# A GNN stack under a list scheduler: layers without order between groups, other ranks, the last groups' steps alternating, and attention terms written to DRAM element by element

## The chip, the cores and the metric

The kernel runs on one core of a Trainium2 chip. The time is device microseconds of one execution. The kernel before takes 1331.21 us, the median of three runs (1329.94 to 1332.13 us).

A core has TensorE (PE, matrix products into PSUM; its weight loads are PEld), VectorE (DVE), ScalarE (ACT), GpSimd (POOL) and SyncE (SP), which here issues nearly all DMAs. Each engine executes its own instructions in the order in which the program holds them and waits on semaphores for the others.

## The reference

128 graphs of 64 nodes with 256 features go through four layers, each after a layer norm and a ReLU, each added to its input:

```python
h = jnp.maximum(_layernorm(x, axis=-1), 0.0)
x = x + _L0_gnn_ref(h, adj, W, a_src, a_dst)    # attention, 4 heads of 64
h = jnp.maximum(_layernorm(x, axis=-1), 0.0)
x = x + _L1_gnn_ref(h, adj, W, a)               # attention, 1 head of 256
h = jnp.maximum(_layernorm(x, axis=-1), 0.0)
x = x + _L2_gnn_ref(h, ...)                     # relational convolution; adj holds only 0 and 1
h = jnp.maximum(_layernorm(x, axis=-1), 0.0)
x = x + _L3_gnn_ref(h, adj, ...)                # gated graph recurrence, 3 steps of a GRU
```

An attention layer forms, for every pair of nodes of a graph and every head, the exponential of a leaky ReLU of the sum of a source term and a destination term, masks it by the adjacency, and averages the neighbours' features with it. A step of the recurrence is

```python
m = h @ weight[i]; aggr = A.T @ m               # per graph
r = sigmoid(i_r + h_r); z = sigmoid(i_z + h_z)  # i_* from aggr @ w_ih.T, h_* from h @ w_hh.T
n = tanh(i_n + r * h_n)
h = (1.0 - z) * n + z * h
```

## The kernel before

**Tiles and stages.** Two graphs fill the 128 partitions; four such pairs are a group, so there are 16 groups (NG). A group first goes through three layers (first_layer, second_layer, third_layer) and then through the three steps of the recurrence. A step (g, i) is step i of group g. A step has 42 products of 128x128 by 256 columns: for each gate a 2x2 block product is done with seven products instead of eight (class Sevens), so POOL forms sums of blocks of the state (hS) and of the aggregated state (aS). PSUM banks "sy" (two) and "sz" (three) hold the results; VectorE and ScalarE empty them. Everything else uses three banks called "mt".

**Who sets the order.** Nothing is emitted as it is written. Every call to an engine is recorded (Plan.note), belongs to a job (Plan.begin, with a start and an end in the plan's own time and a list of jobs that must have ended before), and has a planned cost (the function cost). Plan.emit then makes list schedules: forward takes, among the operations that can start, the one with the smallest due time; backward sets new due times from the end. Of 21 such passes (PASSES) the shortest in the plan's own time is emitted: that fixes the order on each engine. Where the plan leaves TensorE idle in its first 115 us, emit puts filler products "sz<-warm" (L1582).

**Order of steps.** The list steps interleaves two neighbouring groups: (g, 0), (g-1, 2), (g, 1), ... It ends with (14,0), (13,2), (14,1), (15,0), (14,2), (15,1), (15,2). The function when gives each place a slot, and a group's layers end before its first slot. The layers' jobs are chained through users: layer i of a group starts in the plan only when layer i of the group before has ended.

**The way back of the state.** A step leaves the state hT with features on partitions; the next needs it with nodes on partitions too (hnat). If the same group's next step follows at once ("quick"), TensorE transposes it: eight products "tp<-ident,hT" (back). If not, back_by_dma has VectorE transpose 32x32 blocks (tb), writes them to DRAM (way) and reads them back (hnat). The last step of all (final, in_parts) transposes on TensorE, adds the input and stores.

**Attention terms.** For each node and head, fs holds an exponential of the source term, with nodes on partitions. The pair products need it along the free axis in all partitions of the graph (t). From group 2 on (AHEAD) TensorE transposes fs (tp<-ident,fs), VectorE copies it out of PSUM (fT), one DMA writes it to DRAM rows (row<-fT, 32 or 8 pieces of 256 bytes), and two DMAs read the rows, broadcast over 64 partitions, as t. VectorE then multiplies t by gd, takes the maximum with fd and the minimum with the mask mt; TensorE aggregates (mm<-wh,t and mn<-wh,t).

Of the kernel before, what the change touches and what calls it, by code (L numbers as in the profile page):

```python
# [2 lines left out]

# [6 lines left out]
F32 = mybir.dt.float32  # L10
I32 = mybir.dt.int32
AF = mybir.ActivationFunctionType
# [209 lines left out]
class Plan:  # L222
# [54 lines left out]
            b.ops.append(op)  # L277
        return op

    PASSES, SEED, SPREAD = 21, 28, 50.0  # L280
    LEEWAY = {"PE": 100.0, "DVE": 100.0, "Activation": 100.0, "Pool": 100.0, "SP": 300.0, "-": 0.0}
    OVERLAP = {"DVE": 83.0, "Activation": 95.0, "Pool": 43.0}
    ISSUE, TURN = 665.0, 197.0
# [133 lines left out]
    def backward(self, end):  # L417
# [26 lines left out]
        for _ in self.ops:  # L444
# [14 lines left out]
            for other in before[op]:  # L459
                limit(other, op.due - self.LATENCY - other.took)  # L460

    def emit(self):

        self.on = False
        self.link()
        best, self.random = None, Random(self.SEED)
        for _ in range(self.PASSES):
            end, order = self.forward()
            if best is None or end < best[0]:
                best = end, [(op, op.start, op.idle, op.places) for op in order]  # L470
            self.backward(end)
        self.ends = best[0]
        for op, start, idle, places in best[1]:
            op.start = start
            if op.engine == "PE" and self.spare and start < 115.0 * 1e3:
                for _ in range(int((idle - 100.0) / 220.0)):
                    self.spare()
            for b, tag in places:
                b.pool.make(b, tag)
            op.call()  # L480
        self.ops = []
        return best[0]
# [46 lines left out]
def cost(engine, method, args, kwargs):  # L529

    n = elements(args[0])
    if engine == "tensor":
        m = elements(args[2] if method == "matmul" else args[0])
        return (m / 1.2 + 2.5) * (1 if method == "transpose" else 2)
    if engine == "sync" or method == "dma_start":
        to, of = args[:2]
        rate = {"way": 450.0, "fine": 175.0}.get(to.base.tag, 150.0) if isinstance(to, View) else 150.0
        if isinstance(of, View) and of.base.tag in ("way", "fine"):
            rate = 150.0 if of.base.tag == "way" else 100.0
        return n * to.shape[0] * 4 / rate  # L540
    if engine == "vector":
        if method == "bn_stats":
            return 400.0
        if method == "tensor_reduce":
            n = elements(args[1])
        plain = method == "tensor_scalar" and not any(isinstance(a, View) for a in args[2:4])
        return 150.0 + n * (0.53 if plain and n >= 512 else 1.04)
    if engine == "scalar":
        return 150.0 + 0.86 * n if method in ("copy", "mul") else 310.0 + 0.73 * n
    if ALU.pow in args:  # L550
        return 1000.0
    return 200.0 + 2.1 * n if method != "memset" else 100.0 + 0.85 * n
# [3 lines left out]
def kernel(  # L556
# [368 lines left out]
    class Recurrence:  # L925
# [7 lines left out]
        def at(self, x, k, h):  # L933

            return chunk(x, k)[:, 2 * h : 2 * h + 2]
# [69 lines left out]
        def step(self, i, back=True, in_parts=False):  # L1005
# [73 lines left out]
            def gates(c):  # L1079
                g = Sevens(c, "r", (0, 1))  # L1080
                rs, zs = (turned_part(name) for name in "rz")
                r, z = ([x[:, 2 * h : 2 * h + 2] for h in range(2)] for x in (rs, zs))

                def r_there(h, y):
                    nc.scalar.activation(r[h], y, AF.Tanh, bias=brz[:, c : c + 1], scale=0.5)
                    nc.vector.scalar_tensor_tensor(t[c][h], r[h], 1.0, t[c][h], op0=ALU.add, op1=ALU.mult)

                def z_there(h, y):
                    nc.vector.tensor_tensor(z[h], y, z[h], ALU.add)
                    if h == 0:  # L1090
                        nc.scalar.activation(zs, zs, AF.Tanh, bias=brz[:, 2 + c : 3 + c], scale=0.5)

                nc.scalar.copy(r[0], g.mul("y", 1))
                nc.vector.tensor_tensor(r[0], g.mul("m", 2), r[0], ALU.add)
                r_there(0, r[0])
                nc.scalar.copy(z[0], g.mul("y", 6))
                nc.scalar.copy(z[1], g.mul("y", 5))
                z_there(1, g.mul("z", 7))
                r_there(1, g.mul("y", 3))
                z_there(0, g.mul("z", 4))  # L1100
                return r, z, rs, zs
# [5 lines left out]
            def from_a(gated):  # L1107
                n = Sevens(0, "n", (1,))

                def add(c, h, y):  # L1110
                    nc.vector.tensor_tensor(t[c][h], t[c][h], y, ALU.add)

                def there(c, h):
                    d, z, ds, zs = gated[c]
                    nc.scalar.activation(t[c][h], t[c][h], AF.Tanh, bias=bi[:, 4 + c : 5 + c])
                    nc.gpsimd.tensor_tensor(d[h], at(hT, c, h), t[c][h], ALU.subtract)

                add(0, 0, n.mul("y", 1))
                add(0, 0, n.mul("m", 2))
                there(0, 0)  # L1120
                add(1, 0, n.mul("y", 6))
                add(1, 1, n.mul("y", 5))
                add(1, 1, n.mul("z", 7))
                there(1, 1)
                add(0, 1, n.mul("y", 3))
                there(0, 1)
                done(*gated[0][2:], chunk(hnew, 0))
                if back:
                    back_first()
                add(1, 0, n.mul("z", 4))  # L1130
                there(1, 0)
                done(*gated[1][2:], chunk(hnew, 1))

            def back_first():
                self.hT = hnew
# [23 lines left out]
    with ExitStack() as s1:  # L1159
# [47 lines left out]
        class Layer:  # L1207
# [2 lines left out]

            place = {"em": "hn", "dg": "hn", "tb": "hn", "land": "hn"}

            shared = {"hn": 3, "o": 2, "st": 4, "mv": 4, "var": 4, "rstd": 4, "nm": 4, "rec": 4, "fT": 1}

            def __init__(self, layer, pool, bufs):
                self.layer, self.pool, self.bufs = layer, pool, bufs
# [106 lines left out]
        def attention(g, p0, n, layer, heads, we, pool):  # L1323
# [13 lines left out]
            if g < AHEAD:  # L1337

                dg = pool.tile([P, nh, N], F32, name="dg")
                nc.gpsimd.tensor_tensor(  # L1340
                    dg.rearrange("p (g h) i -> p g h i", g=n),
                    diag[:, None, None, :].to_broadcast([P, n, heads, N]),
                    es[:, :, :heads, None].to_broadcast([P, n, heads, N]),
                    ALU.mult,
                )
                step = 512 // N
                for c in range(0, nh, step):
                    m = min(step, nh - c)
                    pe = psum.tile([P, 512], F32, name="mm")
                    nc.tensor.matmul(  # L1350
                        pe[:, : m * N], same, dg[:, c : c + m, :].rearrange("p c i -> p (c i)"), start=True, stop=True
                    )
                    nc.scalar.activation(
                        t[:, c : c + m, :].rearrange("p c i -> p (c i)"), pe[:, : m * N], AF.Exp, scale=ALPHA - 1.0
                    )
            else:

                fs = pool.tile([P, n, heads], F32, name="fs")
                nc.scalar.activation(fs, es[:, :, :heads], AF.Exp, scale=ALPHA - 1.0)
                pt = psum.tile([P, T], F32, name="tp")  # L1360
                nc.tensor.transpose(pt[:nh, :P], fs.rearrange("p g h -> p (g h)"), ident)
                fT = pool.tile([nh, P], F32, name="fT")
                nc.vector.tensor_copy(fT, pt[:nh, :P])
                row = dram.tile([2, nh * N], F32, name=f"row{layer}")
                nc.sync.dma_start(row.rearrange("a (c i) -> c a i", i=N), fT.rearrange("c (a i) -> c a i", i=N))
                for half in range(2):
                    nc.sync.dma_start(
                        t[half * N : (half + 1) * N].rearrange("p c i -> p (c i)"),
                        row[half : half + 1, :].to_broadcast([N, nh * N]),
                    )  # L1370
# [113 lines left out]
        start, slot = 87.96, 27.0  # L1484
        PLAIN = (0, NG - 1)
        steps = [(0, 0), (0, 1)]
        for g in range(1, NG):
            steps += [(g, 0), (g - 1, 2), (g, 1)]
        steps.append((NG - 1, 2))
        turn = {step: n for n, step in enumerate(steps)}  # L1490

        def when(g, i):
            return start + turn[g, i] * slot

        users = {}

        def layers_of(g):
            if g > 1:
# [11 lines left out]
            for p0, n, at in units:  # L1510
                spare = g == 0 and p0 > 0
                for i in range(3):
                    end = None if g < 2 else at[i + 1]
                    nc.begin((g, p0, i), at[i], end, [users[i]] if i in users and not spare else [])
                    if g > 1:
                        nc.job.spread = 3.0
                    if not spare:
                        users[i] = (g, p0, i)
                    layers[i](g, p0, n, spare)
            if g == 0:  # L1520
                nc.begin("make")
# [278 lines left out]
```

## The time and the profile before

| | us |
|---|---|
| median of the runs | 1331.21 |
| profiled execution | 1333.37 |
| its span, first to last instruction | 1331.6 |
| TensorE busy in the span | 1307.7 |
| VectorE busy | 1065.1 |
| ScalarE busy | 859.2 |
| GpSimd busy | 691.5 |
| DMA of queue q1, share of 16 engines | 34.8% |

The span is cut into 40 equal slices; a digit is the busy share of a slice in tenths, and PEclk is the granted clock of TensorE:

```profile
PE   9998999999999999999999999999999999999986
PEld 8666877878788787878778787877878788778875
DVE  6578688897979788796988879697897979777663
ACT  4866667676676767666676666766676666655543
...
PEclk9999999999999999999999999999999999999998
DMA  7110224435343534524253443434335323422210
```

A float32 product shows as two records. Records overlap, since a product's end is modelled, so the distance from one start to the next says more than a record's length. A group of instructions is named output<-inputs with buffer numbers left out; nearly all come from one helper (L495), so groups are told apart by their tiles. "Landing" is the time from a DMA's issue to its end.

### The profile page before, as it was taken

The page shows a single profiled execution, that of the slowest core. Times are in us where ns is not written, and L with a number is a line of the kernel's source. Part 1 is how long each engine was busy: PE and PEld are TensorE (multiplying, and loading weights), DVE is VectorE, ACT ScalarE, POOL GpSimd, SP SyncE. Part 2 cuts the span into 40 slices and gives each one's busy share as a digit, 9 for nine tenths or more (in the row PEclk, how much of TensorE's full clock was granted, in tenths as well). Part 3 has the DMA queues.
Part 4 walks back from the last instruction along what each step waited for, and adds up shares of the span by engine and source line. Part 5 has one row for each costly group of instructions (what it writes and reads, how often), then busy time and mean ns, then how long its engine had stood idle before and what let it go on. Part 6 is the DMA issues. An engine that isn't in the chain of part 4 may idle for free.

```text
span 1331.6 us, 27942 instructions
## 1 busy us (share of the span) xinstructions
PE 1307.7 (98%) x9889; PEld 1039.4 (78%) x9889; DVE 1065.1 (80%) x2556; ACT 859.2 (65%) x2173; POOL 691.5 (52%) x845
## 2 busy tenths in 40 slices
PE   9998999999999999999999999999999999999986
PEld 8666877878788787878778787877878788778875
DVE  6578688897979788796988879697897979777663
ACT  4866667676676767666676666766676666655543
POOL 2664553655565355554645455654555546453642
PEclk9999999999999999999999999999999999999998
DMA  7110224435343534524253443434335323422210
GB/s 215 28 36 25 80 85 152 123 101 166 104 124 96 157 114 125 155 94 133 84 159 112 124 148 103 134 98 151 100 115 164 101 90 91 142 66 56 98 54 20
DMA packets 132061, 143.90 MB, mean 108 GB/s; under 512 B 43336, under 2 KB 117320, under 8 KB 131912
## 3 DMA queue, kind: packets, MB, share of 16 engines
q1 hardware_dynamic: 131352, 141.50, 34.8%
q8 instruction: 81, 1.33, 0.4%
q14 instruction: 68, 0.56, 0.1%
q10 hardware_dynamic: 560, 0.52, 0.1%
HBM read 80.48 MB, written 60.96 MB: 106 GB/s over the span
## 4 chain that ended last, share of the span: by engine, by line
PE 93%; DVE 3%; ACT 2%; POOL 1%; issue 0%; DMA 0%; SPq 0%; DVEq 0%; POOLq 0%
PE sy L495 37%; PE sz L495 28%; PE mm L495 17%; PE mm L787 4%; PE tp L787 3%; PE sz L1582 2%; PE tp L495 1%; DVE hT L495 1%; PE tq L787 1%; ACT hn L495 1%; DVE r L495 0%; PE mn L787 0%; DVE t L495 0%; DVE st L495 0%; ACT z L495 0%
## 5 line engine op out<-in xcount | busy, mean ns | idle before, releaser
L495 POOL TENSOR_TENSOR r<-hT,hT 128x256 f32<-128x256 f32 x192 | 152.2, 799 | 266.1 <-ACT hT L495 265.2
L495 DVE SCALAR_TENSOR_TENSOR hT<-r,hT 128x256 f32<-128x256 f32 (+1 forms) x288 | 181.6, 635 | 39.2 <-ACT r L495 37.0
L495 PE MATMUL sy<-hS,wsum 128*128 128x256 f32 x576 | 173.4, 384 | 1.0 <-ACT z L495 0.6
L495 PE MATMUL sy<-aS,wsum 128*128 128x256 f32 x576 | 173.0, 383 | 0.0
L495 PE MATMUL sz<-hS,whh 128*128 128x256 f32 x576 | 170.5, 383 | 0.1
L495 PE MATMUL sz<-aS,wc 128*128 128x256 f32 x576 | 164.7, 383 | 0.0
L495 DVE TENSOR_TENSOR hT<-hT,sz 128x256 f32<-128x256 f32 x288 | 118.2, 411 | 54.7 <-PE sz L495 48.3
L495 POOL TENSOR_TENSOR aS<-aT 128x256 f32<-128x256 f32 x96 | 80.9, 843 | 150.8 <-ACT aT L495 150.6
L495 ACT ACTIVATE hT<-sy,bh 128x256 f32<-128x256 f32 x192 | 90.6, 472 | 68.8 <-PE sy L495 66.4
L495 PEld LDWEIGHTS sy<-hS,wsum 128*128 128x128 f32 x576 | 107.1, 191 | 30.3 <-issue 8.8
L495 ACT ACTIVATE hT<-hT,bi 128x256 f32<-128x256 f32 x192 | 95.3, 505 | 50.9 <-DVE hT L495 49.5
L495 PEld LDWEIGHTS sz<-hS,whh 128*128 128x128 f32 x576 | 107.1, 190 | 23.2 <-issue 7.4
L495 PEld LDWEIGHTS sy<-aS,wsum 128*128 128x128 f32 x576 | 107.2, 190 | 19.7 <-issue 3.2
L495 PEld LDWEIGHTS sz<-aS,wc 128*128 128x128 f32 x576 | 106.5, 190 | 18.4 <-issue 1.2
L495 POOL TENSOR_TENSOR rstd<-var,mhalf 128x4 f32<-128x4 f32 (+1 forms) x70 | 74.9, 1070 | 82.6 <-ACT var L495 78.1
L495 PE MATMUL mm<-wl,hT 128*128 128x512 f32 x248 | 117.5, 593 | 0.0
L495 ACT ACTIVATE hn<-xg,nm,rstd 128x256 f32<-128x256 f32 x200 | 107.2, 593 | 10.7 <-POOL nm L495 10.2
L495 ACT COPY z<-sy 128x256 f32<-128x256 f32 x192 | 70.7, 369 | 66.4 <-PE sy L495 65.0
L495 DVE TENSOR_TENSOR hT<-hT,sy 128x256 f32<-128x256 f32 x192 | 79.6, 414 | 32.6 <-PE sy L495 30.2
L495 DVE TENSOR_TENSOR z<-sz,z 128x256 f32<-128x256 f32 x192 | 79.7, 416 | 32.3 <-PE sz L495 27.5
L495 DVE SCALAR_TENSOR_TENSOR r<-z,r 128x512 f32<-128x512 f32 x96 | 89.0, 929 | 13.8 <-ACT z L495 7.6
L495 DVE BATCH_NORM_STATS2 st<-xg 128x6 f32<-128x256 f32 x256 | 95.8, 409 | 3.2 <-DMA xg<-in_x_dram 3.1
(207 smaller groups left out, 3228.7 us busy)
## 6 DMA issues: line engine op xcount, KB each, us to landing
way<-tb SPq DMA_DIRECT2D x58, 512.0 KB, 2.7
hnat<-way SPq DMA_DIRECT2D x180, 128.0 KB, 2.9
way<-hn SPq DMA_DIRECT2D x42, 512.0 KB, 3.0
hn<-way SPq DMA_DIRECT2D x168, 128.0 KB, 3.0
xg<-in_x_dram SPq DMA_DIRECT2D x15, 512.0 KB
out_dram<-xg SPq DMA_DIRECT2D x15, 512.0 KB, 2.9
t<-row SPq DMA_DIRECT2D x28, 256.0 KB, 4.0
hT<-way SPq DMA_DIRECT2D x52, 128.0 KB, 2.6
```

Of the source, the lines that this page charges most:

```text
L495: return do(*[real(a) for a in args], **{k: real(v) for k, v in kwargs.items()})
L787: nc.nc.tensor.matmul(*[real(x) for x in product], start=True, stop=True)
L1582: nc.spare = lambda: psum.spare and nc.nc.tensor.matmul(pause, warm, warm, start=True, stop=True)
```

## The change

It does six things.

- The list users is gone: a layer's job no longer waits for the same layer of the group before.
- The last steps alternate: (14,0), (13,2), (15,0), (14,1), (15,1), (14,2), (15,2). No step of group 15 follows another of it at once, so (15,1) brings its state back by DMA and not on TensorE.
- Due times are shifted: 50 passes and not 21, from another seed; then 125 recorded random moves (MOVES), each of which shifts the due times of some jobs, in a stretch of the plan, on some or all engines, and one more forward pass whose order is emitted.
- Planned costs of DMAs of the tags "way" and "fine" are other numbers.
- In the last step, the tanh of z and the function done work on halves (256 columns) instead of on both at once (512).
- From group 2 on, fs goes to the DRAM rows straight from its 128 partitions: two DMAs, one for each graph of the pairs, in which every element is a piece of 4 bytes (1024 pieces each in the first layer, 256 in the second). The transposes of fs, the copies fT and their tile are gone.

```diff
-    PASSES, SEED, SPREAD = 21, 28, 50.0
+    PASSES, SEED, SPREAD = 50, 3, 50.0
+    MOVES = (
+        3000014, 3000022, 3000028, 3000041, 3000063, 3000064, 3000083, 3000087, 3000102, 3000106, 3000107, 3000112,
...
+    RANKED = ("PE", "DVE", "Activation", "Pool", "SP")
+
+    def move(self, seed, end, jobs):
...
+        u()
+        middle = u() * end
+        width = (15e3 if u() < 0.5 else 50e3) * (0.3 + u())
+        by = (60.0, 200.0, 600.0, 2000.0)[int(u() * 4)]
+        together = int(u() * 3) == 0
+        for j in jobs:
+            if not abs(j.sum / j.count - middle) < width or u() < 0.5:
+                continue
+            if together:
+                d = shift(by)
+                for e in self.RANKED:
+                    j.shift[e] += d
+            else:
+                for e in self.RANKED:
+                    if u() >= 0.5:
+                        j.shift[e] += shift(by)
...
         for _ in range(self.PASSES):
+            ranks = [op.due for op in self.ops]
             end, order = self.forward()
             if best is None or end < best[0]:
-                best = end, [(op, op.start, op.idle, op.places) for op in order]
+                best = end, ranks, [op.start for op in self.ops]
             self.backward(end)
+        end, ranks, starts = best
...
+        for m in self.MOVES:
+            self.move(m, end, jobs)
+        for op, due in zip(self.ops, ranks):
+            op.due = due + op.job.shift.get(op.engine, 0.0)
+        end, order = self.forward()
+        best = end, [(op, op.start, op.idle, op.places) for op in order]
...
-        rate = {"way": 450.0, "fine": 175.0}.get(to.base.tag, 150.0) if isinstance(to, View) else 150.0
+        rate = {"way": 450.0, "fine": 220.0}.get(to.base.tag, 150.0) if isinstance(to, View) else 150.0
         if isinstance(of, View) and of.base.tag in ("way", "fine"):
-            rate = 150.0 if of.base.tag == "way" else 100.0
+            rate = 170.0 if of.base.tag == "way" else 125.0
...
                     nc.vector.tensor_tensor(z[h], y, z[h], ALU.add)
-                    if h == 0:
+                    if in_parts:
+                        nc.scalar.activation(z[h], z[h], AF.Tanh, bias=brz[:, 2 + c : 3 + c], scale=0.5)
+                    elif h == 0:
                         nc.scalar.activation(zs, zs, AF.Tanh, bias=brz[:, 2 + c : 3 + c], scale=0.5)
...
                     nc.gpsimd.tensor_tensor(d[h], at(hT, c, h), t[c][h], ALU.subtract)
+                    if in_parts:
+                        done(d[h], z[h], t[c][h])
...
-                done(*gated[1][2:], chunk(hnew, 1))
+                if not in_parts:
+                    done(*gated[1][2:], chunk(hnew, 1))
...
-                pt = psum.tile([P, T], F32, name="tp")
-                nc.tensor.transpose(pt[:nh, :P], fs.rearrange("p g h -> p (g h)"), ident)
-                fT = pool.tile([nh, P], F32, name="fT")
-                nc.vector.tensor_copy(fT, pt[:nh, :P])
                 row = dram.tile([2, nh * N], F32, name=f"row{layer}")
-                nc.sync.dma_start(row.rearrange("a (c i) -> c a i", i=N), fT.rearrange("c (a i) -> c a i", i=N))
+
+                def scatter():
+                    with nc.allow_non_contiguous_dma(reason="attention terms to rows"):
+                        for a in range(2):
+                            nc.sync.dma_start(
+                                real(row)[a].rearrange("(c i) -> i c", i=N),
+                                real(fs)[a * N : (a + 1) * N].rearrange("p g h -> p (g h)"),
+                            )
+
+                nc.note("SP", scatter, 150.0 * nh, [row], [fs], dma=True)
...
-        for g in range(1, NG):
+        for g in range(1, NG - 1):
             steps += [(g, 0), (g - 1, 2), (g, 1)]
-        steps.append((NG - 1, 2))
+        steps[-1:] = [(NG - 1, 0), (NG - 2, 1), (NG - 1, 1), (NG - 2, 2), (NG - 1, 2)]
...
-        users = {}
-
...
-                    nc.begin((g, p0, i), at[i], end, [users[i]] if i in users and not spare else [])
+                    nc.begin((g, p0, i), at[i], end)
                     if g > 1:
                         nc.job.spread = 3.0
-                    if not spare:
-                        users[i] = (g, p0, i)
```

Counted in the built programs, TensorE loses 28 transposes of fs, 8 of the state and 18 filler products (106 to 88), VectorE loses 28 copies, gains two block transposes and has eight half-size operations in place of four whole ones, and SP has 33 DMAs more.

## The prediction

> **What bounds the kernel now.** I read the page's busy shares first, then the windows of the span, then TensorE's timeline where a window was not full.
>
> ```profile
> PE 1307.7 (98%) x9889; PEld 1039.4 (78%) x9889; DVE 1065.1 (80%) x2556; ACT 859.2 (65%) x2173; POOL 691.5 (52%) x845
> ...
> 0.00:99.60 99.60, 96.78 (x671) 73.09 (x671) 63.27 (x189) 64.10 (x203) 47.52 (x88) 1.00 0.33 93
> ...
> 126.20:136.20 10.00, 5.89 (x33) 3.95 (x36) 9.93 (x20) 6.53 (x14) 9.86 (x10) 0.92 0.00 0
> 136.20:1292.50 1156.30, 1153.42 (x8788) 922.01 (x8788) 952.36 (x2257) 761.01 (x1895) 613.95 (x721) 1.00 0.37 115
> 1292.50:1304.30 11.80, 8.19 (x88) 6.62 (x88) 4.96 (x7) 4.51 (x10) 5.88 (x8) 0.71 0.14 46
> ```
>
> From 136 to 1292 us TensorE is busy for 1153.4 of 1156.3 us: there only less TensorE work makes the kernel faster. Time that isn't work lies at three places: before the first recurrence product, in the turn from step (0,0) to (0,1), and in the turn from (15,1) to (15,2). TensorE's timeline shows the last of them, and the form list shows three groups that only fill or move data:
>
> ```profile
> 1296.28 1.09 PE L495 MATMUL tp<-ident,hT 128*128 128x128 f32 x4 [3.61 <-DVE hT L495]
> 1297.16 1.91 PE L495 MATMUL sy<-hT,whh 128*128 128x256 f32 x4
> ...
> 1303.30 0.70 PE L495 MATMUL sy<-hS,wsum 128*128 128x256 f32 x2
> ...
> L1582 PE MATMUL sz<-warm 128*128 128x128 f32 x212 | 29.3, 289 | 1.1 <-DVE warm L1580 1.1
> ...
> L495 PE MATMUL tp<-ident,fs 128*16 128x128 f32 x14 | 3.8, 273 | 0.0
> L495 PE MATMUL tp<-ident,fs 128*4 128x128 f32 x14 | 3.8, 273 | 0.0
> ```
>
> TensorE waits 3.61 us for VectorE's state, and then four records take 1.91 us where elsewhere eight take 1.73: the bubble is followed by products at half rate.
>
> **What the Trainium skill says.** "TensorE: Matmul & The Clock Gate", "What's actually happening": after an idle window of about 3.4 us the clock falls to half until a busy window has passed. The trace agrees: after the 3.61 us bubble a record's pitch is about 0.43 us until about 1302, against 0.216. "DMA: Bandwidth & Descriptors", "Rules for kernel authors": a last dimension that is not contiguous gives one descriptor per element, and "Specifications" there names read-modify-write below 512 B. The one such transfer of before, the two bias loads (1536 pieces of 4 bytes around 27 us), shows no such penalty on reads; 4-byte writes to DRAM don't occur in before.
>
> ```profile
> DMA packets 942, 0.01 MB, mean 13 GB/s; under 512 B 942, under 2 KB 942, under 8 KB 942
> ## 3 DMA queue, kind: packets, MB, share of 16 engines
> q1 hardware_dynamic: 942, 0.01, 86.8%
> ...
> DMA to landing us min/median/max: 1.3/1.3/2.2
> ```
>
> The first three lines are 27.0 to 27.6 us: 942 packets in 0.6 us on 16 engines is one per 16 x 600 / 942 = 10.2 ns and engine. The last is row<-fT, 32 pieces of 256 bytes in layer 0 and 8 in layer 1.
>
> **The change, part by part.** A 256-wide record has a pitch of 0.216 us (eight in 1.73), a product has two; a 128-wide transpose has (1.09 - 0.27) / 7 = 0.117 us (eight hn transposes at 129.97).
>
> 1. *Rows without TensorE.* From group 2 on, 28 transposes of fs leave TensorE: 28 x 0.117 = 3.3 us, in the stretch that is full, so it counts in full. VectorE loses 28 copies of 272 ns, 7.6 us of an 80% busy engine. SP gets 28 more issues; a bias issue with 768 pieces took 516 ns. Chain: in layer 0 of the 14 visits, read off the timeline, the row issue came 2.2 us after fs started (TensorE, then VectorE had to get to it), the issue of t 1.8 us later, 3.9 together. Now: fs 0.23 and a hop of 0.1, first issue 0.52, then for the second half 64 pieces per engine at 10.2 ns, 0.65, and the 1.3 us of row<-fT: 2.8 us, about 1 us earlier. Write pieces are the unknown: at the read price the chain gains, and it is neutral at (3.9 - 1.6) / 128 = 18 ns a piece. I take the read price, since 256-byte row writes also land in 1.3 us, and book the shorter chain at nothing: products of t follow 14 to 18 us of other products in both orders. SP's queue behind the wait for fs holds way<-tb and hnat<-way of the running recurrence, as it did behind fT.
>
> 2. *Last steps alternate.* Before, (15,1) and (15,2) follow each other. From 1292.5 to 1304.3 TensorE has 88 records: 64 of the aggregation (one burst of about 1.1 us), 8 transposes, 16 records of 0.216 = 3.5 us. Useful 4.6 of 11.8 us; lost 7.2, transposes and half clock included. Now (14,2) with 42 products, 42 x 0.43 = 18 us, lies between, and the state returns by DMA: two block transposes (0.7 us each), way and hnat (2.7 and 2.9 us to landing), under 10 us with issues. It fits, as it does in every earlier step, so I count 7.2 us. What is late next is group 15's layers, wanted a slot earlier; in the new order their last products stand at 1095 us of TensorE work against 1109 before, so they have moved along.
>
> 3. *New order at the head.* Summing products at their pitches over the two built orders, the first recurrence product stands after 66.8 us of work and 106 filler products (0.222 us each, 23.5 us) before, and starts at 99.6: 9.3 us are neither. After the change it stands behind 76.4 us of work and 88 fillers, 19.5 us. Fillers are put where the plan has TensorE idle. With the same 9.3 us the head loses 28.8 instead of 32.8: 4.0 us gained.
>
> 4. *Turn (0,0) to (0,1).* 126.2 to 136.2 us: 12 records of 0.216 and 16 transposes make 4.5 us of work in 10 us, 5.5 lost. In the new order eight hn transposes and five w1e products (0.9 + 2.2 us) stand ahead of the first state product, and three more w1e products and a layer-0 aggregation (1.3 + 0.6 us) ahead of the last four state transposes. I take 4.0 of the 5.5.
>
> 5. *The last step in halves.* Tanh of z on 256 columns instead of 512 saves 0.2 us, and two VectorE operations of 0.69 become 0.43 each; but a 0.68 us hnat addition now stands ahead of the last one on VectorE. 0.3 us.
>
> 6. *Layers free of each other, shifted ranks, "fine" rates.* No tile has the tag "fine"; the way rate only moves the order. In the full stretch nothing can be gained but the 3 us of gaps; new orders bring waits of their own. Before has five gaps of 0.7 to 1.4 us from one product to the next there (at 193, 685, 929, 1023 and 1090 us); I book 3 us more, between -3 and +8.
>
> Sum: -3.3 - 7.2 - 4.0 - 4.0 - 0.3 + 3.0 = -15.8. The profiled execution was 1333.4 us with a span of 1331.6, so 1.8 lie around it; the median of the runs, 1331.2, is 2.2 below it. 1331.2 - 15.8 = 1315.
>
> **The rivals.**
> - *The model's fill does not come (items 3 and 4 fail).* Fillers are placed by the kernel's own plan, not by a measurement; loads and VectorE could be late as before. For: VectorE is 9.93 of 10 us busy in the turn at 126 us, so it may still decide there. Against: layer products that need nothing of it stand in between now. Then -3.3 - 7.2 - 0.3 + 3 = -7.8: 1323.
> - *The 4-byte writes are slow: slower than before.* Place: VectorE's first multiplication of t, which waits for t<-row; behind it stand the recurrence's PSUM readers, then TensorE. Price: each ns per piece beyond 18 costs 128 x 14 = 1.8 us over the 14 layer-0 visits. At 18 + 15.8 / 1.8 = 27 ns the gain is gone, at 28 the kernel is 0.2% slower, at 40 ns it takes 1331 - 16 + 40 = 1355. For: all pieces of one column lie side by side in the same lines of DRAM, written by all engines, and the skill's read-modify-write. Against: the read price of 10 ns, and a 256-byte write's quick landing.
> - *New waits eat the gain.* Freed layers crowd the buffers; 16 us over 1156 us would be one 0.25 us gap per 18 us. Against: TensorE's products still have 14 us of others ahead of them. 1331.
>
> **How the numbers follow.** Main case 0.61, at 1315, own range 1308 to 1321 (items 2 to 4 all full, or interior +8). First rival 0.21, at 1323. Slow writes 0.12. Eaten 0.06. A measurement of this kernel can tell 0.2%, 2.7 us: faster is the main case and the first rival, 0.82; same 0.06; slower 0.12. The range leaves out the slow writes and a little at each end: 1306 to 1330.
>
> **What would show it.** In the new profile: no tp<-ident,fs and no fT; row<-fs landing in 2 to 3 us after its issue; 0 to 100 us with 76 us of work before the first sy product at about 104 us; no gap over 1 us with half clock between 1270 and the last step; VectorE's waits for t<-row at a few us in all, as the 1.7 us before. Wrong would be: waits for t<-row of tens of us and DMA shares near full around row<-fs (slow writes), or the middle stretch under 99% busy (new waits).

## The result and the profile after

The changed kernel takes 1516.82 us (median of five runs, 1514.23 to 1519.35) beside 1330.83 for the kernel before (five runs in turn with it, 1329.94 to 1332.13): a ratio of 1.1397, interval 1.1381 to 1.1414. It is 14% slower; the forecast was 1315.

The page of the profile after, its busy times, its slices, its DMA queues and its chain of work that ended last:

```profile
PE 1363.2 (90%) x9817; PEld 1067.0 (70%) x9817; DVE 1068.8 (70%) x2534; ACT 858.6 (57%) x2173; POOL 698.7 (46%) x845
...
PE   9988897988988889798887988789898997989997
...
q1 hardware_dynamic: 167968, 142.55, 36.4%
...
PE 61%; DMA 19%; DVE 9%; ACT 4%; issue 4%; POOL 2%; SPq 1%; another core or an unknown queue 0%; DVEq 0%; ACTq 0%; POOLq 0%
PE sy L553 23%; PE sz L553 18%; PE mm L553 12%; DMA row<-fs 10%; DMA t<-row 4%; DMA way<-tb 3%; PE mm L845 3%; DVE hT L553 2%; DVE t L553 2%; PE tp L845 2%; SPq L553 1%; PE sz L1647 1%; ACT hT L553 1%; PE tp L553 1%; DMA xg<-in_x_dram 1%
```

(The helper is L553 now, the aggregation L845.) VectorE, ScalarE and GpSimd have nearly the same work as before. The DMA engines' share is hardly higher (q1 36.4% of the span beside 34.8%), and yet DMA holds 19% of the chain, where it held 0% before. One window of the span, first of the kernel before, then of the changed one, gives the place; the columns are the busy times of PE, PEld, DVE, ACT and POOL with their instructions, PEclk, DMA share and GB/s:

```profile
136.20:1275.00 1138.80, 1135.92 (x8707) 906.88 (x8708) 940.58 (x2231) 753.31 (x1878) 606.62 (x714) 1.00 0.38 115
136.20:1275.00 1138.80, 1011.02 (x7332) 790.38 (x7331) 795.40 (x1868) 642.33 (x1609) 513.39 (x600) 0.93 0.39 98
```

In this stretch TensorE is idle for 127.8 us, where it was for 2.9 us before, and its granted clock is 0.93 on average. Bubbles are followed by half clock, and here it doesn't take one of 3.4 us, the figure that the prediction cites: around a bubble of 2.48 us (263.2 to 265.7 us) the clock is 0.50 from 265.4 to 268.8. The waits name the transfer (us in total, times, longest): VectorE's for t, then those in SyncE's queue for the rows, each before (L495) and after (L553):

```profile
DVE t L495 <- DMA t<-row: 1.7, 4, 0.7
DVE t L553 <- DMA t<-row: 122.5, 23, 15.0
...
SPq L495 <- DMA row<-fT: 24.4, 23, 2.9
SPq L553 <- DMA row<-fs: 202.9, 32, 10.5
```

SyncE's timeline shows one visit of each attention layer, first one of layer 1 (two writes of 256 pieces), then one of layer 0 (two of 1024); the columns are start, length and tiles:

```profile
319.89 1.25 SPq L553 DMA_DIRECT2D row<-fs  x2
321.25 0.55 SPq L553 DMA_DIRECT2D way<-tb  x1
...
329.84 2.22 SPq L553 DMA_DIRECT2D t<-row  x2
332.17 1.00 SPq L553 DMA_DIRECT2D hnat<-way  x2
...
350.71 1.34 SPq L553 DMA_DIRECT2D row<-fs  x2
361.97 1.13 SPq L553 DMA_DIRECT2D t<-row  x2
```

The reads of t are issued 10.0 and 11.3 us after the first of the rows' writes; in the first visit the state's way back, hnat<-way, stands behind them in the same queue. In the visit of layer 0 the DMA engines are not at work all that time. The DMA line of the window 350.7 to 362 us, in 40 slices of 0.28 us:

```profile
DMA  0000276573000000000000000000050000000000
...
q1 hardware_dynamic: 2080, 0.01, 8.2%
```

The 2048 pieces go through the engines between 352.0 and 353.4 us. The queue's next transfer is issued only 8.6 us later (the mark in between is a fetch of instructions): the writes are through the engines but have not landed. In the visit of layer 1 a write of the state, way<-tb, was issued behind the pieces, and there the engines do show as busy (319.8 to 330 us):

```profile
DMA  0230040043999990000000900000168431140666
...
q1 hardware_dynamic: 1109, 0.62, 79.2%
```

The 128 packets of 4096 bytes in this window, the state's, take 0.91 us each on average; such packets take 0.18 us in the kernel before. So other writes behind the pieces are slow as well.

### The profile page after: what moved, and what is told of

Same layout as the page of the kernel before. It is cut to its first block, busy times and chain, and to the rows that moved or that the text cites. A ratio compares the mean times of both kernels' runs of the same rounds, so it can differ in the third digit from the quotient of the medians.

```text
span 1517.5 us, 27822 instructions
## 1 busy us (share of the span) xinstructions
PE 1363.2 (90%) x9817; PEld 1067.0 (70%) x9817; DVE 1068.8 (70%) x2534; ACT 858.6 (57%) x2173; POOL 698.7 (46%) x845
## 3 DMA queue, kind: packets, MB, share of 16 engines
q1 hardware_dynamic: 167968, 142.55, 36.4%
## 4 chain that ended last, share of the span: by engine, by line
PE 61%; DMA 19%; DVE 9%; ACT 4%; issue 4%; POOL 2%; SPq 1%; another core or an unknown queue 0%; DVEq 0%; ACTq 0%; POOLq 0%
PE sy L553 23%; PE sz L553 18%; PE mm L553 12%; DMA row<-fs 10%; DMA t<-row 4%; DMA way<-tb 3%; PE mm L845 3%; DVE hT L553 2%; DVE t L553 2%; PE tp L845 2%; SPq L553 1%; PE sz L1647 1%; ACT hT L553 1%; PE tp L553 1%; DMA xg<-in_x_dram 1%
## 5 line engine op out<-in xcount | busy, mean ns | idle before, releaser
L553 POOL TENSOR_TENSOR r<-hT,hT 128x256 f32<-128x256 f32 x192 | 152.2, 799 | 364.1 <-ACT hT L553 359.4
L553 PE MATMUL sy<-aS,wsum 128*128 128x256 f32 x576 | 184.8, 407 | 30.5 <-DVE hT L553 26.4
L553 DVE SCALAR_TENSOR_TENSOR hT<-r,hT 128x256 f32<-128x256 f32 (+1 forms) x290 | 183.7, 637 | 24.1 <-ACT r L553 21.9
L553 PE MATMUL sy<-hS,wsum 128*128 128x256 f32 x576 | 179.4, 397 | 9.7 <-ACT z L553 6.9
L553 PE MATMUL sz<-hS,whh 128*128 128x256 f32 x576 | 178.4, 395 | 8.2 <-DVE hT L553 4.1
L553 PE MATMUL sz<-aS,wc 128*128 128x256 f32 x576 | 169.9, 391 | 5.1 <-DVE hT L553 5.1
L553 PEld LDWEIGHTS sy<-aS,wsum 128*128 128x128 f32 x576 | 112.8, 201 | 60.8 <-DVE hT L553 32.3
L553 DVE TENSOR_TENSOR hT<-hT,sz 128x256 f32<-128x256 f32 x288 | 118.3, 411 | 40.0 <-PE sz L553 31.1
L553 ACT ACTIVATE hT<-hT,bi 128x256 f32<-128x256 f32 x192 | 95.9, 504 | 86.4 <-DVE hT L553 85.5
L553 PEld LDWEIGHTS sy<-hS,wsum 128*128 128x128 f32 x576 | 109.6, 196 | 40.3 <-ACT z L553 10.7
L553 ACT ACTIVATE hT<-sy,bh 128x256 f32<-128x256 f32 x192 | 90.5, 472 | 83.6 <-PE sy L553 74.4
L553 PEld LDWEIGHTS sz<-hS,whh 128*128 128x128 f32 x576 | 111.4, 197 | 32.0 <-issue 9.7
L553 POOL TENSOR_TENSOR aS<-aT 128x256 f32<-128x256 f32 x96 | 83.8, 873 | 103.2 <-ACT aT L553 97.5
L553 PEld LDWEIGHTS sz<-aS,wc 128*128 128x128 f32 x576 | 111.4, 196 | 25.4 <-DVE hT L553 5.9
L553 DVE TENSOR_TENSOR t<-t,gd 128x512 f32<-128x512 f32 (+2 forms) x48 | 28.4, 603 | 131.5 <-DMA t<-row 122.5
L553 PE MATMUL mm<-wl,hT 128*128 128x512 f32 x248 | 119.2, 594 | 0.0
L553 ACT ACTIVATE hn<-xg,nm,rstd 128x256 f32<-128x256 f32 x200 | 108.9, 594 | 17.2 <-POOL nm L553 16.4
L553 POOL TENSOR_TENSOR rstd<-var,mhalf 128x4 f32<-128x4 f32 (+1 forms) x70 | 77.8, 1111 | 87.3 <-ACT var L553 82.9
L553 ACT COPY z<-sy 128x256 f32<-128x256 f32 x192 | 70.7, 369 | 78.3 <-PE sy L553 74.9
L845 PE MATMUL mm<-wh,t 64*64 64x65 f32 (+1 forms) x620 | 54.3, 301 | 63.9 <-DVE t L553 62.9
L553 DVE TENSOR_TENSOR hT<-hT,sy 128x256 f32<-128x256 f32 x192 | 79.7, 415 | 41.5 <-PE sy L553 39.5
L553 DVE TENSOR_TENSOR z<-sz,z 128x256 f32<-128x256 f32 x192 | 79.7, 416 | 40.5 <-PE sz L553 34.2
```

The source lines that it names most:

```text
L553: return do(*[real(a) for a in args], **{k: real(v) for k, v in kwargs.items()})
L845: nc.nc.tensor.matmul(*[real(x) for x in product], start=True, stop=True)
```

## The experiments

Edits are shown as short diffs against the kernel named, with "..." where lines are left out; e1 to e16 stand for the full labels (there is no e10).

### Is it the writes? e1, e2, e3

*e1_rows_by_transpose*: the changed kernel with the rows' old way.

```diff
+                pt = psum.tile([P, T], F32, name="tp")
+                nc.tensor.transpose(pt[:nh, :P], fs.rearrange("p g h -> p (g h)"), ident)
+                fT = pool.tile([nh, P], F32, name="fT")
+                nc.vector.tensor_copy(fT, pt[:nh, :P])
...
-                nc.note("SP", scatter, 150.0 * nh, [row], [fs], dma=True)
+                nc.sync.dma_start(row.rearrange("a (c i) -> c a i", i=N), fT.rearrange("c (a i) -> c a i", i=N))
```

> The changed kernel with the old way of the attention terms put back (transpose on TensorE, copy fT, one DMA of 256-byte pieces); all else of the change kept. Theory W (the 4-byte writes land late and hold up t): the loss is gone and what is left of the change shows, 1331 - 12.5 = 1318, between 1310 and 1326. Theory O (the new order and the freed layers cost the time, the pieces are a bystander): still 1400 or more.

*e2_pieces_only*: the kernel before, with the reverse of this edit. *e3_pieces_unread*: e1 with the same scatter added, into rows of its own that nothing reads.

> The kernel before with the 4-byte pieces alone, all else as before. Theory W: t comes 6 to 8 us late at 28 visits, 1470 to 1530. Theory O: 1320 to 1340.

> e1_rows_by_transpose with the 4-byte pieces issued as well, into rows that nobody reads. If the damage is only that t waits for its rows (theory W, direct): within 10 us of e1, below 1330. If the pieces also hold up other DRAM writes (way, hnat) in the rings (theory W, crowding): 1360 to 1450, with long waits for DMA way<-tb.

Measured: e1 1350.98 us (ratio 1.0143, interval 1.0126 to 1.0160), e2 1536.62 (1.1543, 1.1520 to 1.1566), e3 1497.65 (1.1251, 1.1228 to 1.1273). The writes alone make the kernel before 15% slower, and writes that nobody waits for still cost e3 147 us over e1. The waits of e3, engines first and then SyncE's queue:

```profile
POOL xg L553 <- DMA hnat<-way: 95.8, 11, 24.4
DVE t L553 <- DMA t<-row: 92.4, 20, 9.3
...
SPq L553 <- DMA row<-fT: 119.5, 21, 10.4
```

In e1 these were 12.6 us, 3.5 us and 17.4. So ordinary writes behind the pieces land late too. e3 lies above the range expected for crowding, and of the sign expected there, waits for way<-tb, VectorE shows 25.6 us beside 1.1 in e1. e3 also puts 56 more issues in SyncE's queue; e13 below has as many more than e8 and is no slower, so they don't explain the 147 us. e2 is 7 us above its range. e1 fell between both theories: without the pieces the change loses 1.4% still. That is taken up in the third group.

### What is slow about such a write? e4, e5, e16

Writes appended to the kernel before, each read back by a small read before the next goes out; the distance from the issue of a write to that of its read is its landing. In *e4_layouts* they were moved to the start of the program, ran beside its loads and not in turn: 1357.21 us, and nothing to be read from it.

> The kernel before, followed by 18 writes from SBUF to DRAM one after the other, each read back before the next, so that the distance from a write's issue to its read's issue is its landing: 64 pieces of 64 bytes; 64x16, 64x4 and 64x1 pieces of 4 bytes laid side by side as in the change; 64x16 with 8 bytes from piece to piece, all of a partition together; 64x16 and 64x4 with 64 bytes from piece to piece; 64x16 with 512 bytes; and both halves as in the change. Its time is longer by these writes and says nothing. Theory L (pieces of different DMA engines in the same DRAM line queue up): side by side 7 to 10 us for 64x16 and nearly as long for 64x4, but 2 to 3.5 us wherever a line belongs to one engine or one piece. Theory C (every 4-byte write has its price): 64x16 side by side and at 64 bytes alike, 7 to 10 us, and 64x4 a quarter of the excess, about 3 to 4 us.

*e5_layouts_in_turn* has them behind the last instruction, so its 1540.35 us mean nothing.

```diff
+            written((space.tile([N, 4], F32, name=f"run16_{again}"), h0[:, :4]))
+            written((flat(f"col16_{again}", 16 * N).rearrange("(c i) -> i c", i=N), h0[:, :16]))
+            written((flat(f"col4_{again}", 4 * N).rearrange("(c i) -> i c", i=N), h0[:, :4]))
...
+            written((space.tile([N, 4, 16], F32, name=f"own64x4_{again}")[:, :, 0], h0[:, :4]))
+            written((space.tile([N, 16, 128], F32, name=f"own512_{again}")[:, :, 0], h0[:, :16]))
```

> The kernel before with a series of writes appended after its last instruction, each read back by one small read before the next begins, so that the time from a write's issue to the issue of its read is the write's landing; the series runs twice. Nothing of the output changes. All writes go from 64 partitions to DRAM. With pieces of 4 bytes side by side, as in the change: 16 columns (1024 pieces), 4 columns (256), 1 column (64). With pieces of 4 bytes set apart: 1024 pieces at steps of 8, 64 and 512 bytes, 256 at a step of 64. With runs: 64 runs of 64 bytes, 64 of 16 bytes. Then both halves as in the change (2 x 1024), the same with an ordinary write of 64-byte runs behind them, and the same with two small reads of an older row behind them. Theory L (pieces that share a stretch of DRAM are written one after the other): side by side 7 to 10 us with 4 columns nearly as long as 16, and those at steps of 64 and 512 bytes like the runs, 2 to 3.5 us. Theory C (a fixed price for each piece): the steps of 8, 64 and 512 bytes take as long as side by side, and 4 columns a quarter of the excess of 16. Under both, if other transfers are held up, the write behind the pieces lands several us later than the runs alone, and the two reads take longer than twice the usual 2 us.

SyncE's timeline, in this order: 64 runs of 16 bytes; 1024 and 256 pieces side by side; 256 pieces set 64 bytes apart; 1024 set 512 bytes apart:

```profile
1334.19 0.48 SPq L495 DMA_DIRECT2D run<-piece_src  x1
1335.86 0.46 SPq L495 DMA_DIRECT2D piece_src<-run  x1
1338.15 0.64 SPq L495 DMA_DIRECT2D col<-piece_src  x1
1349.25 0.46 SPq L495 DMA_DIRECT2D piece_src<-col  x1
1351.41 0.61 SPq L495 DMA_DIRECT2D col<-piece_src  x1
1358.67 0.45 SPq L495 DMA_DIRECT2D piece_src<-col  x1
...
1383.96 0.54 SPq L495 DMA_DIRECT2D own64x<-piece_src  x1
1385.88 0.45 SPq L495 DMA_DIRECT2D piece_src<-own64x  x1
1387.69 0.54 SPq L495 DMA_DIRECT2D own<-piece_src  x1
1390.41 0.45 SPq L495 DMA_DIRECT2D piece_src<-own  x1
```

Landings of 1.67, 11.10, 7.26, 1.92 and 2.72 us; the second round differs by at most 0.4 us. As many pieces of 4 bytes, set apart, land in a quarter of the time: it is not a price for each piece (theory C), it is where they lie. 64 pieces side by side still took 6.8 us, 1024 at steps of 8 bytes 5.0 and 5.7 us. The transfers put behind a pair of such writes told nothing: the reads that end them overwrite the pair's source, and so waited for the pair itself.

*e16_one_line* asked how it grows:

```diff
+            for k in (1, 2, 4, 8, 16, 32, 64):
+                one(flat(f"line{k}_{again}", k).rearrange("(c i) -> i c", c=1), src[:k, 0:1], k)
...
+            one(flat(f"byrow_{again}", 16 * N).rearrange("(c i) -> i c", i=N), old)
+            one(flat(f"bycol_{again}", 16 * N).rearrange("(c i) -> c i", i=N), old.rearrange("i c -> c i"), 16)
```

> Again the kernel before with writes appended that are read back one by one. 1, 2, 4, 8, 16, 32 and 64 pieces of 4 bytes from as many partitions, side by side in DRAM; then the change's 1024 pieces; a plain write of 64-byte runs; and that block turned from DRAM to DRAM in pieces of 4 bytes, once in the order of its source and once in the order of its target. If each further piece in a stretch of 64 bytes waits for the one before: the time rises by some 0.3 us with each piece up to 16 (about 1.7, 2.0, 2.6, 3.9, 6.5 us) and hardly after that. If it is the number of pieces: 64 takes four times the excess of 16. If it is pieces of several DMA engines that collide: the turn in the order of its target lands in some 3 us, in the order of its source like the change's.

The timeline for 16, 32 and 64 pieces side by side, and for the turn from DRAM to DRAM in the order of its target:

```profile
1338.13 0.31 SPq L495 DMA_DIRECT2D line<-piece_src  x1
1339.41 0.31 SPq L495 DMA_DIRECT2D piece_src<-line  x1
1342.19 0.30 SPq L495 DMA_DIRECT2D line<-piece_src  x1
1345.35 0.30 SPq L495 DMA_DIRECT2D piece_src<-line  x1
1349.05 0.52 SPq L495 DMA_DIRECT2D line<-piece_src  x1
1355.36 0.49 SPq L495 DMA_DIRECT2D piece_src<-line  x1
...
1381.01 0.60 SPq L495 DMA_DIRECT2D bycol<-old  x1
1390.30 0.32 SPq L495 DMA_DIRECT2D piece_src<-bycol  x1
```

1.28, 3.16, 6.31 and 9.29 us; 1 to 8 pieces took 1.0 to 1.2 us (the very first write, 3.3), 1024 as in the change 9.4, the turn in its source's order 7.7 and 8.7. None of the three pictures holds: 16 pieces in 64 bytes side by side cost next to nothing, 64 of them 5 us more, which is far above four times that, and the order over the target doesn't help. What is shown is the condition, many pieces of 4 bytes close together in DRAM: side by side 16 land fast and 32 don't, and 1024 at steps of 8 bytes are slow as well. What in the way to the memory takes the time stays open.

### What is the rest of the change worth? e6, e9, e11, e12

*e6_transpose_no_moves* is e1 with `for m in ():` in place of `for m in self.MOVES:`. The others are the kernel before with one thing of the change: *e9_last_steps_only* the alternation and the last step in halves, *e11_freed_only* no list users, *e12_other_seed* 50 passes from seed 3.

> The first experiment's kernel (all of the change, but attention's terms reach the rows by transpose) without the 125 shifts of ranks. Theory M (the shifts are fitted to the graph with the pieces and disorder the one with the transposes): 1315 to 1335 us, the idle time between 200 and 1275 us back to some 3 us per 100. Theory O (layers free of each other's jobs, or the alternation of the last steps, cost the middle stretch): 1345 to 1360 us, as with the shifts.

> The kernel before with the alternation of the last two groups' steps and the last step in halves, nothing else of the change. The prediction's items 2 and 5: 7.5 us less, 1323 us, with no idle stretch around 1280 to 1300 us. Rival (the plan is made anew for the whole program, and a new order loses by new waits in the middle): 1331 to 1340 us, the turn's idle time gone but returned between 200 and 1275 us.

> The kernel before with the layers free of each other's jobs, nothing else of the change. If freeing them costs waits: 1340 us or more, with the waits where group g's layer work and the step that reads it meet. If it only gives the planner another order: 1325 to 1338 us.

> The kernel before with the planner's passes and seed of the change (50 and 3 in place of 21 and 28): the same graph and costs in another order. If the order alone is worth several us: 1333 to 1345 us, with idle time spread between 200 and 1275 us. If it is worth nothing: within 0.2% of before.

| | median us | ratio to before, interval | TensorE not busy, 136.2 to 1275 us |
|---|---|---|---|
| e1, with the shifts | 1350.98 | 1.0143 (1.0126 to 1.0160) | 20.1 |
| e6, without | 1335.54 | 1.0032 (1.0021 to 1.0044) | 11.9 |
| e9, last steps | 1327.07 | 0.9972 (0.9961 to 0.9982) | 4.2 |
| e11, freed | 1330.61 | 0.9997 (0.9987 to 1.0008) | 5.1 |
| e12, seed | 1334.09 | 1.0018 (1.0009 to 1.0028) | 3.0 |

The 125 shifts cost 15 us on a graph (the operations and what each waits for) that has the transposes; on the graph without them they gain (e15 below). They are 15 of e1's 20 us; the other 5 are not traced to a part. Freeing the layers fills the turn at 126 us (10.00 of 10 us busy) but loses as much elsewhere: nothing by itself. The alternation gives 1331 x 0.0028 = 3.7 us, half of what was booked. Another seed is worth 2.4 us in the wrong direction, with the middle as full as before. The planned costs of the tags "way" and "fine" were not tried by themselves.

### The change without the slow writes: e7, e14, e8, e13, e15

*e7_runs_node_major* lays the rows out by node, so that each partition writes one run, and turns the tile t instead. *e14_node_major_again* is the same kernel, run once more; the trace read below is its.

```diff
...
-                                real(row)[a].rearrange("(c i) -> i c", i=N),
+                                real(row)[a].rearrange("(i c) -> i c", c=nh),
...
```

> The changed kernel with the rows laid out by node in place of by column: each partition writes one run (64 bytes in layer 0, 16 in layer 1) in place of 16 or 4 pieces of 4 bytes, and t is read with a stride. Same recorded work, ranks and shifts as the changed kernel. Theory W (the pieces' writes cost all of the loss): row issue to t issue 2 to 3.5 us, and 1305 to 1325 us. Theory O (the order and the freed layers cost too): 1335 to 1360 us with short chains. If strided reads of t cost, VectorE's sums over t take longer than the changed kernel's and the time lies up to 15 us above.

> The kernel of e7_runs_node_major once more, for its records: t is laid out by node and read with a stride of 64 bytes (16 in layer 1). If strided reads cost, VectorE's operations on t take longer than in e8_runs_unturned, or the weight loads and products of t do, by some 34 us in all on the path, with the rows' landing near 2 us in both.

*e8_runs_unturned* has this edit alone, and t is read as before: the work is the same, but the terms stand in another order in t, so its output is not the reference's.

> The changed kernel with the same number of bytes written into each row, but as one run per partition (64 bytes in layer 0, 16 in layer 1) and read by t as if it had been written by column: the terms reach t in another order of nodes and heads, so the attention weights are those of permuted terms. Everything else, the order on every engine and the tiles' layouts included, is the changed kernel's; e5_layouts_in_turn measured 1.7 us for the landing of such runs. Theory W (writing pieces side by side is all that is wrong with the change): 1305 to 1325 us, the prediction's sum. Theory O (the change's order and its freed layers lose too, as e6_transpose_no_moves showed for its own order): 1335 to 1360 us, near e7_runs_node_major's 1355; then the strided reads of t in e7 cost nothing.

e7 took 1354.91 us (1.0187, 1.0165 to 1.0210), e14 1352.31 in one run, e8 1320.48 (0.9911, 0.9891 to 0.9931). Between the changed kernel and e8 nothing differs but the form of the write: 196 us. What e7 pays beyond e8, 34 us, shows in the groups of instructions by form (busy us, mean ns). First e8:

```profile
L845 PEld LDWEIGHTS mm<-wh,t 64*64 64x64 f32 x620 | 24.4, 133 | 27.0 <-issue 9.3 <-PE sy L553 5.9 <-PE sz L553 5.8
...
L553 DVE TENSOR_TENSOR t<-t,mt 128x512 f32<-128x512 f32 x31 | 22.8, 739 | 0.1
L553 DVE TENSOR_TENSOR t<-t,fd 128x512 f32<-128x512 f32 x31 | 21.9, 715 | 0.0
```

and e14, with t read at a stride:

```profile
L850 PEld LDWEIGHTS mm<-wh,t 64*64 64x64 f32 x620 | 42.2, 193 | 33.0 <-issue 13.0 <-PE sy L558 8.0 <-DVE t L558 4.4
...
L558 DVE TENSOR_TENSOR t<-t,fd 128x512 f32<-128x512 f32 x31 | 35.1, 1144 | 0.0
...
L558 DVE TENSOR_TENSOR t<-t,mt 128x512 f32<-128x512 f32 x31 | 32.9, 1066 | 0.2
```

Weight loads from t take 193 ns and not 133, VectorE's operations on it 1.1 us and not 0.7. How the 34 us divide between the two was not measured.

*e13_block_transposes* keeps the layout of the rows and turns the terms on VectorE; ScalarE first writes them as 32 columns. The Trainium skill says in "VectorE: DVE Perf Modes", section "The three transpose paths", that VectorE transposes blocks of 32x32 only, SBUF to SBUF; that is enough here, since four blocks of 32 nodes give runs of 32 x 4 = 128 bytes. Here one took 201 ns (28 of them, 5.6 us).

```diff
...
+                    nc.nc.vector.transpose(ft, real(fs))
+                    for b in range(P // 32):
+                        half, j = divmod(32 * b, N)
+                        nc.nc.sync.dma_start(
+                            real(row)[half].rearrange("(c i) -> c i", i=N)[:, j : j + 32],
+                            ft[32 * b : 32 * b + nh, :],
+                        )
...
```

> The changed kernel with its terms turned by VectorE: exp writes 32 columns per partition, one VectorE transpose of 32 x 32 blocks per visit, and four writes of 16 (layer 1: 4) runs of 128 bytes replace the two writes of 4-byte pieces. The order on every engine is the changed kernel's but for the 28 added VectorE operations and two more issues per visit on SyncE. Theory W (only pieces side by side are bad): landing 2 to 3 us, and 1320 to 1328 us, at most 8 us above e8_runs_unturned: 28 VectorE operations of some 0.2 to 0.3 us and 28 x 2 issues of 0.5 us, mostly off the path. Theory S (SyncE's longer queue or VectorE's extra waits count): 1328 to 1340 us.

*e15_blocks_no_shifts* is e13 without the shifts of ranks.

> The kernel of e13_block_transposes without the 125 shifts of ranks: the graph of the change in the planner's own order. If the shifts are worth something where they fit: 1322 to 1335 us, with the idle time between 136 and 1275 us above e13's 4.9 us or the head and turn less full. If the planner's own order is as good: 1312 to 1319 us, and then the shifts only do harm where the graph is another one.

e13 takes 1315.40 us: 0.9882, interval 0.9866 to 0.9899. Unlike e8 it does the reference's computation, and it is faster than the kernel before and the changed one. e15 takes 1333.70 (1.0018, 1.0009 to 1.0027): the shifts are worth 18 us where they fit. e13's page, then two of its windows:

```profile
PE 1296.6 (99%) x9817; PEld 1031.3 (79%) x9817; DVE 1075.0 (82%) x2562; ACT 856.8 (65%) x2173; POOL 704.9 (54%) x845
...
PE 87%; DVE 3%; POOL 1%; ACT 1%; issue 1%; DMA 0%; SPq 0%; DVEq 0%; POOLq 0%; ACTq 0%
```

```profile
126.20:136.20 10.00, 10.00 (x142) 8.45 (x141) 5.53 (x11) 6.70 (x21) 8.09 (x10) 1.00 0.03 10
136.20:1275.00 1138.80, 1133.92 (x8598) 908.59 (x8597) 940.63 (x2195) 743.31 (x1843) 619.23 (x714) 1.00 0.36 112
```

The turn is full, the middle lacks 4.9 us, and VectorE waits 6.4 us in all for t<-row.

## Why the prediction was wrong

**The step that failed** is in item 1: "at the read price the chain gains ... I take the read price, since 256-byte row writes also land in 1.3 us". The chain from the issue of the rows to that of t was to take 0.52 + 0.65 + 1.3 us; it took mostly 11.5 in layer 0 and 7.5 to 10.2 in layer 1. The packets did pass at 7 to 9 ns each, about the price that the bias loads suggested, but their time in the engine is not their landing. The kernel before shows no write of that form, and I took a price that transfers of two other forms suggested.

Two things in the same item were put at nothing and were not. The chain was booked at nothing because "products of t follow 14 to 18 us of other products"; but VectorE waited 122.5 us for t at its first multiplication of it, with the recurrence's PSUM readers behind that in its order. And SyncE's queue was to hold the way back of the state no longer than "it did behind fT"; it waited 202.9 us for the rows, where it had waited 24.4.

**The rival that was right was too small.** "The 4-byte writes are slow" had the place and the wait, and a chance of 0.12. Of its two signs the waits for t<-row came; the DMA shares near full did not in layer 0's window (8.2%), and came in layer 1's (79%), where another write stood behind the pieces. Its price was wrong in three ways. It was per piece, so that layer 1 with a quarter of the pieces seemed harmless, while e5 shows 256 side by side at 7.3 us and 1024 at 11.1. It counted only what t's own wait costs, while e3 loses 147 us with nobody waiting for the pieces, through ordinary writes and reads behind them. And 40 ns was an upper end with no run behind it: 196 us over 28 visits is 7.0 us per visit.

What the rival rested on, the read-modify-write below 512 B in the Trainium skill's "DMA: Bandwidth & Descriptors", section "Specifications", is seen in no run here and doesn't decide by itself: runs of 16 bytes (1.7 us in e5) and of 128 (t issued mostly 1.5 to 3 us after the rows in e13) are below 512 too. The bad case is narrower: many 4-byte pieces close together.

**The rest of the sum held in total, once the writes are mended, but in part by luck.** Against e13 (16.2 us faster by its medians, span 19.4 shorter):

| item | booked | found in e13's records, unless named |
|---|---|---|
| 1, rows without TensorE | -3.3 | the 28 transposes are gone; not measured by itself |
| 2 and 5, last steps | -7.5 | -3.7 by e9 alone; the 3.61 us bubble is gone, and the time from the last recurrence product to the end falls from 12.0 to 9.3 us |
| 3, head | -4.0 | first recurrence product at 104.9 us (forecast about 104), with 176 filler records and not 212 (-36 x 0.111 = -4.0) |
| 4, turn | -4.0 | 10.00 of 10 us busy at full clock: the whole 5.5 |
| 6, middle | +3.0 | 4.9 us not busy and not 2.9: +2.0 |

With e9's figure these add to -14.5: the alternation gave half of what was booked, the turn 1.5 us more, the middle cost 1.0 less, and 1 to 2 us of e13's gain belong to no item. That e13's 1315.4 meets the 1315 is so partly luck. In the changed kernel itself the turn is not filled (5.73 of 10 us busy in 126.2 to 136.2 us). Where the order got its quality was not seen: I booked nothing for the shifts as such and read their effect off the built order, which came out for the sum; e15 shows that without them the same graph is no faster than before.

## What to carry to other kernels

A transfer that a kernel has never made is not priced by one in the other direction: ask for the landing of that very form, measured by reading it back, before a chain rests on it. Where DRAM has to hold data turned, make runs on the chip first; one VectorE transpose in 32x32 blocks, 0.2 us a visit, made 128-byte runs in place of writes that cost 7 us a visit. And an order found for one graph is a property of that graph: the same shifts gave 18 us on it and cost 15 us on its neighbour.

## What was not expected of the hardware

- A write is late long after its packets: 2048 pieces were through the engines in 1.4 us and landed about 11 us after their issue.
- Side by side, 16 pieces of 4 bytes land in 1.3 us, 32 in 3.2, 64 in 6.3, 256 in 7.3 and 1024 in 9.3 to 11.1; 256 set 64 bytes apart land in 1.9.
- Transfers behind them are slow as well: packets of 4096 bytes took 0.91 us each behind 512 such pieces and 0.18 in the kernel before, and pieces that nobody reads cost e3 147 us.
- The share of busy DMA engines shows this only where something stands behind the pieces: 8.2% in the one window, 79% in the other.
